# Local attention with whitening on one core: the first softmax's transposes move into image 1's infinity row, and its band transposes are held back

## Chip, cores and metric

The kernel runs on one core of one Trainium2 chip. The metric is device time in microseconds (us) of one execution; lower is better. TensorE is called PE below, VectorE DVE, ScalarE ACT, GpSimd POOL, and SP is the sync engine that issues most transfers.

## The reference

Input x has four images of 256 channels, 64 x 64. Layer 0 makes 49 attention weights for each pixel and sums the pixel's 49 neighbours with them; layer 1 whitens the channels.

```python
k = conv(x, w1, 7x7, dilation 2, padding 6) + b1        # 256 -> 128 channels
k = conv(k, w2, 1x1) + b2                               # 128 -> 49
attn = softmax(k, axis=1)
y = sum over u, v of shift(x, 2u, 2v) * attn[7u + v]    # local attention
# layer 1, in groups of 64 channels, over all pixels of all images
Sigma = EPS * I + cov(y);  P = 5 Newton steps towards Sigma^(-1/2)
out = (P * sqrt(1 / trace)) @ (y - mean) * weight + bias
```

## The kernel before

**Convolution.** The two convolutions are folded into one with 49 outputs. It is done by evaluation and interpolation, in both directions of the image: seven points 0 to 5 and infinity (INF). A *row* below is one row point `br` of one image. For a row, `row_eval` forms combinations of image rows (buffers `rb`), `col_ops` those of columns (`xh`, temporaries `ct`), `weights` the transformed filters (`wr`), and `conv_bank` multiplies them on PE in three banks (`BANKS`, `i` = 0, 1, 2) into the PSUM buffers `cv`. ACT evicts each bank to `pv`, `col_interp` interpolates columns to `zz` and `row_interp` interpolates rows to the logits, in the tile `lgx` (image 0: in `slot` 4). The bias of the logits is added by ACT on line 658. `row_interp` runs in two parts, after rows 4 and 5.

Some rows are computed by plain taps instead: `direct` walks 14 pairs of tap and channel half. Image 0 uses it for rows 0, 4, 5 and INF, the others for INF alone (`direct_inf`, whose taps come from the DRAM tile `gi` into `spare`, the third buffer of `pv`). A `direct` with `s` = 1 adds its result to the half that was there before: a copy on ACT and a sum on DVE (line 690 and the line after it). Image 1's INF row is the exception: it is called with the taps still in SBUF and accumulates in `acc`, before image 1's weights of banks 1 and 2 are prepared.

**Attention.** `soft(b, pc)` takes half the pixels of image b: PE transposes the logits, DVE takes maxima, ACT exponentiates, DVE normalizes. `move_terms` copies the result to `zt` and stores it to the DRAM tile `sd`; `load_band` reads it back, shifted, into `band` in three parts, four transfers each, and DVE block-transposes each part (line 973). `first_half(n)` and `second_half(n)` then multiply on PE the transposed image blocks with `band` (line 1020); n counts half-pixel quarters of images, four to an image.

**Order.** PE follows the order of the code (`keep_in_program_order`). On the other engines and queues a scheduler orders instructions by priority and by its own estimate of when they are ready; `high_priority` raises a block. While `strict` is set, `in_turn` keeps the DVE operations of `add`, `sub` and `madd` in code order. `later` holds ACT copies that are let go behind the next eviction of a bank 1. The list `steps` gives the order of the rows of images 1 to 3, with costs 6, 5 and 2 for the three banks of a row; the attention of earlier images is put into gaps of this list by `plan`. In image 1 the list begins with `soft(0, 0)`, three banks of its first row, and `soft(0, 1)`.

`prepare(k, i)` makes what bank i of row k needs (weights, row and column combinations) and is called while row k - 1 is multiplied. Rows 4 and 5 of image 0 leave their row-transformed filters in DRAM (`kept`); image 1 loads them to `rb[0]` when it makes its weights from them.

Of the kernel before, what the change touches and what calls it, by code (L numbers as in the profile page):

```python
# [10 lines left out]
AF = mybir.ActivationFunctionType  # L11
# [21 lines left out]
def kernel(  # L33
# [244 lines left out]

    TT, STT = nc.vector.tensor_tensor, nc.vector.scalar_tensor_tensor

    turn, strict = [None], [False]

    def in_turn(ins):


        if turn[0] is not None:
            tc.add_manual_dep(
                ins.ins,
                turn[0],
                mybir.DependencyInfo(mybir.DependencyClass.NoSync, mybir.DependencyReason.DATA),  # L290
                reason="in_turn",
            )
        if strict[0]:
            turn[0] = ins.ins.name
        return ins
# [68 lines left out]
    def weights(b, br, i, mid=None):  # L364
# [16 lines left out]
        if br == 0:  # L381
            g = [gr0[:, v] for v in range(KS)]
        elif br in kept:

            f = rb[0].rearrange("p q r c w -> p (q r c w)")[:, : KS * nk]
            if i == 0:
                nc.sync.dma_start(f, kept[br])
            f = f.rearrange("p (v a r k) -> p v a r k", v=KS, a=NCC, k=KT)
            g = [f[:, v] for v in range(KS)]
        else:  # L390
            g = [gbr[:, v] for v in range(KS)]
# [249 lines left out]
    def row_interp(b, part):  # L641

        pt = {k: zz[:K2, k] for k in range(NP)}
        lg = lgx
        if b == 0:
            lg = store[4].rearrange("p c r w -> p (c r w)")
        lg = lg[:, : SH * W].rearrange("p (r w) -> p r w", w=W)
        outs = phases(lg[:K2])
        cut = lambda t, k: t[:, k : k + Q8]
        tr = ct.rearrange("p a b -> p (a b)")[:K2, : Q9 * W].rearrange("p (q w) -> p q w", w=W)  # L650
        interpolate(pt, tr, outs, cut, part)
        if part == 0:
            done_ = ((0, outs[0]), (2, outs[2]))
        else:
            done_ = ((3, cut(pt[5], 0)), (1, outs[1]))
            logits[b] = lg
        for a, t in done_:
            nc.scalar.activation(outs[a], t, AF.Identity, bias=bias[:K2])

    logits = {}  # L660

    def direct(b, br, s, ps, w, xr=None):


        a = 3 if br == INF else 0
        order = [(v, cc) for v in sorted(range(KS), key=lambda v: abs(v - R)) for cc in range(NCC)]
        for j, (v, cc) in enumerate(order):
            d = 2 * (v - R)
            w0, w1_ = max(0, -d), min(W, W - d)
            for h in range(2):  # L670
                if xr is None:
                    xs = slots[2 * b + h].rearrange("p c (q a) w -> p a q c w", a=4)[:, a]
                else:
                    xs = xr[:, :, h]
                pe(
                    nc.tensor.matmul(  # L676
                        ps[h * HB : h * HB + KT, :, w0:w1_],
                        w[v][:, cc],
                        xs[:, :, cc, w0 + d : w1_ + d],
                        start=(j == 0),  # L680
                        stop=(j == len(order) - 1),
                        skip_group_check=True,
                    )
                )
        z = zz[:K2, br]
        if s == 0:
            with tc.high_priority():
                nc.scalar.copy(z[:, :Q8], ps[:K2])
        else:
            nc.scalar.copy(z[:, Q8], ps[:K2, Q8 - 1])  # L690
            add(z[:, 1:Q8], z[:, 1:Q8], ps[:K2, : Q8 - 1])

    def conv_psum():
        ncv[0] += 1
        return cv_buf[(ncv[0] - 1) % 2].rearrange("p (q w) -> p q w", w=W)

    def direct_inf(b):

        nc.sync.dma_start(spare[:, :NTAP], kept[INF])
        t = spare[:, :NTAP].rearrange("p (v a k) -> p v a k", v=KS, a=NCC)  # L700
        direct(b, INF, 0, conv_psum(), [t[:, v] for v in range(KS)])

    acc = ps_y.tile([P, 2, Q8, W], F32, tag="y", name="acc")
    nc.vector.memset(acc, 0.0)
    rows = [(0, br) for br in (1, 2, 3)]
    NR0 = len(rows)
    rows += [(b, br) for b in range(1, B) for br in ROWS]
    cur, nxt = {}, {}

    def prepare(k, i):  # L710

# [3 lines left out]
            cur["x"] = row_eval(b, br)  # L715
        nxt.update(w)
        col_eval(cur["x"], i)

    def conv_step(k, i):
        w = {bc: nxt.pop(bc) for bc in BANKS[i]}  # L720
# [76 lines left out]
    for i in three:  # L797
        bank(2, i)
    row_weights(4)
    keep_weights(4)  # L800
    xrs[4] = row_eval(0, 4)
    direct0(4, 0)
# [18 lines left out]
    prepare(NR0, 0)  # L821
    direct0(5, 1)
    row_interp(0, 1)

    direct(1, INF, 0, acc[:, 0], [tap[:, UPOS[3], v] for v in range(KS)])
    prepare(NR0, 1)
    prepare(NR0, 2)
    strict[0] = False
# [120 lines left out]

    BAND = ((0, 3), (3, 5), (5, 8))  # L950

    def load_band(n, part):

        if (n, part) in loaded or n not in moved:
# [4 lines left out]
        for g in range(CR):  # L959
# [6 lines left out]
                ),  # L966
            )

        f = band.rearrange("p m r w -> p (m r) w")[
            :, m0 * BP + (R if m0 == 0 else 0) : m1 * BP - (R if m1 == NCH else 0)  # L970
        ].rearrange("p e w -> p (e w)")
        with tc.high_priority():
            nc.vector.transpose(f, f)  # L973
        if (n, part) == (4 * B - 1, len(BAND) - 1):
            bring_back(dma)

# [231 lines left out]
    for b in range(1, B):  # L1208
# [4 lines left out]
                for i, cost in enumerate((6, 5, 2)):  # L1213
                    steps.append((cost, lambda k=k, i=i: conv_step(k, i)))
        if b == 1:
            steps.insert(0, (0, lambda: soft(0, 0)))
            steps.insert(4, (0, lambda: soft(0, 1)))
        else:
            steps.insert(0, (12, lambda b=b: direct_inf(b)))
        j, at, whole = 0, 0, sum(c for c, _ in steps)  # L1220
        for cost, f in steps:
            f()
            at += cost
            if at * NPC >= (j + 1) * whole:
                gap(b, j)
# [220 lines left out]
```

## Time and profile before

| quantity | value |
|---|---|
| runs | 752.46, 752.98, 753.97 us (median 752.98) |
| profiled execution: its own time, span | 753.07 us, 751.3 us |
| mean granted TensorE clock | 0.984 of full speed |
| matmul instructions, DVE, ACT | 7512, 1268, 953 |
| HBM read, written | 65.88 MB, 47.33 MB |

The profile is of one execution. A line of a timeline is: start in us from the span's start, duration in us, engine, source line, operation, tiles written and read, shape, count, and in brackets the idle time of the engine just before, with what ended it. Lines 306, 309 and 313 are the helpers `add`, `sub` and `madd`, so their operations are told apart by tiles: `xh` column combinations, `ct` their temporaries, `rb` row combinations, `wr` weights, `pv` and `zz` interpolation. Line 536 is a bank's matmuls, 676 those of `direct`, 859 the softmax's transposes, 960 the band's transfers, 973 its block transposes, 932 the store `sd<-zt`, 699 the load of INF taps.

### The profile page before, as it was taken

The page shows a single profiled execution, that of the slowest core. Times are in us where ns is not written, and L with a number is a line of the kernel's source. Part 1 is how long each engine was busy: PE and PEld are TensorE (multiplying, and loading weights), DVE is VectorE, ACT ScalarE, POOL GpSimd, SP SyncE. Part 2 cuts the span into 40 slices and gives each one's busy share as a digit, 9 for nine tenths or more (in the row PEclk, how much of TensorE's full clock was granted, in tenths as well). Part 3 has the DMA queues.
Part 4 walks back from the last instruction along what each step waited for, and adds up shares of the span by engine and source line. Part 5 has one row for each costly group of instructions (what it writes and reads, how often), then busy time and mean ns, then how long its engine had stood idle before and what let it go on. Part 6 is the DMA issues. An engine that isn't in the chain of part 4 may idle for free.

```text
span 751.3 us, 18491 instructions
## 1 busy us (share of the span) xinstructions
PE 706.7 (94%) x7512; PEld 531.5 (71%) x7512; DVE 611.5 (81%) x1268; ACT 332.3 (44%) x953; POOL 50.9 (7%) x52
## 2 busy tenths in 40 slices
PE   6999999997988997999999999999999889998996
PEld 1449643376887795599998976899998678885331
DVE  3799899998999988877997799799969665545575
ACT  1424240253564354375453443745435573322564
POOL 0410070020000110001000100000000000000000
PEclk9999999999999998999999999999999999999999
DMA  8981120127153393046743930433532243362588
GB/s 322 257 302 73 60 88 17 64 98 232 64 183 120 103 342 97 21 132 217 256 130 116 336 82 1 146 111 110 166 90 82 50 135 111 117 251 118 209 359 327
DMA packets 59629, 114.41 MB, mean 152 GB/s; under 512 B 22887, under 2 KB 42008, under 8 KB 58776
## 3 DMA queue, kind: packets, MB, share of 16 engines
q1 hardware_dynamic: 55848, 94.36, 37.7%
q0 software_dynamic: 3696, 18.88, 7.3%
q8 instruction: 59, 0.97, 0.5%
q14 instruction: 26, 0.21, 0.1%
HBM read 65.88 MB, written 47.33 MB: 151 GB/s over the span
## 4 chain that ended last, share of the span: by engine, by line
PE 60%; DVE 27%; ACT 5%; DMA 4%; issue 3%; SPq 1%; DVEq 0%; ACTq 0%
PE cv L536 18%; PE y L1020 13%; PE acc L676 6%; PE tp L1386 4%; PE sig L1073 3%; PE tp L1052 3%; PE cv L676 3%; PE tp L991 3%; DVE xh L313 3%; DVE pv L313 2%; DVE rb L313 2%; DVE zz L313 2%; DMA band<-sd 2%; DVE band L973 2%; PE cv L222 2%
## 5 line engine op out<-in xcount | busy, mean ns | idle before, releaser
L536 PE MATMUL cv<-xh,wr 128*49 128x128 f32 x4368 | 249.7, 275 | 5.9 <-DVE xh L306 5.6
L536 PEld LDWEIGHTS cv<-xh,wr 128*49 128x49 f32 x4368 | 243.6, 124 | 9.9 <-issue 7.1
L1020 PE MATMUL y<-band,xb 128*128 128x224 f32 (+2 forms) x640 | 154.6, 381 | 8.7 <-ACT xb L999 6.7
L1020 PEld LDWEIGHTS y<-band,xb 128*128 128x128 f32 x640 | 111.4, 196 | 31.4 <-ACT xb L999 9.4
L546 ACT COPY pv<-cv 113x486 f32<-113x486 f32 (+1 forms) x63 | 30.0, 476 | 84.6 <-PE cv L536 84.4
L1039 ACT ACTIVATE slot<-y,pivot 128x512 f32<-128x512 f32 x53 | 36.7, 740 | 67.5 <-PE y L1020 67.4
L1060 ACT COPY yt<-tp 128x256 f32<-128x256 f32 x128 | 45.5, 379 | 37.8 <-PE tp L1052 36.4
L973 DVE STREAM_TRANSPOSE band<-band 128x864 f32<-128x864 f32 (+1 forms) x48 | 47.6, 992 | 13.2 <-DMA band<-sd 13.1
L991 PE MATMUL tp<-ident,slot 128*128 128x128 f32 x256 | 50.0, 297 | 8.2 <-ACT yt L1060 8.2
L313 DVE SCALAR_TENSOR_TENSOR pv<-pv 113x162 f32<-113x162 f32 x186 | 55.2, 320 | 0.8 <-ACT pv L546 0.3
L1052 PE MATMUL tp<-ident,slot 128*128 128x128 f32 x256 | 52.0, 299 | 3.7 <-ACT yt L1060 1.0
L1052 PEld LDWEIGHTS tp<-ident,slot 128*128 128x128 f32 x256 | 41.2, 205 | 13.8 <-issue 4.0
L991 PEld LDWEIGHTS tp<-ident,slot 128*128 128x128 f32 x256 | 40.1, 205 | 14.8 <-ACT yt L1060 9.7
L873 ACT ACTIVATE d<-tp,mx 128x49 f32<-128x49 f32 x128 | 36.9, 337 | 21.4 <-DVE mx L868 17.9
L919 ACT COPY zt<-d 32x112 f32<-32x112 f32 (+2 forms) x156 | 44.8, 287 | 1.9
L313 DVE SCALAR_TENSOR_TENSOR xh<-ct 128x512 f32<-128x512 f32 x42 | 27.9, 685 | 13.7 <-PE cv L536 13.4
L1073 PEld LDWEIGHTS sig<-yt 128*64 128x64 f32 x1024 | 33.2, 140 | 6.4 <-issue 4.9
L1073 PE MATMUL sig<-yt 128*64 128x65 f32 x1024 | 37.7, 228 | 0.0
L999 ACT COPY xb<-tp 128x256 f32<-128x256 f32 x87 | 30.5, 375 | 14.0 <-PE tp L991 13.4
L999 DVE COPY xb<-tp 128x256 f32<-128x256 f32 x41 | 16.4, 421 | 23.4 <-PE tp L991 23.4
L676 PE MATMUL acc<-slot,tap 128*49 128x496 f32 (+3 forms) x168 | 34.6, 569 | 0.0
L873 ACT ACTIVATION_READ_ACCUMULATOR d<-tp,mx 128x1 f32 x128 | 30.8, 242 | 0.0
(222 smaller groups left out, 958.0 us busy)
## 6 DMA issues: line engine op xcount, KB each, us to landing
out_dram<-out SPq DMA_DIRECT2D x32, 512.0 KB, 3.4
sd<-zt SPq DMA_DIRECT2D x16, 896.0 KB, 4.0
slot<-in_x_dram POOLq DMA_DIRECT2D x12, 1024.0 KB, 10.1
band<-sd SPq DMA_DIRECT2D x128, 84.0 KB, 2.1
wr<-gd SPq DMA_DIRECT2D x15, 588.0 KB, 3.7
wr<-gd SPq DMA_DIRECT2D x15, 490.0 KB, 4.0
spill<-slot POOLq DMA_DIRECT2D x3, 2048.0 KB, 7.7
back<-spill SPq DMA_DIRECT2D x3, 2048.0 KB, 13.1
```

What stands on the lines that cost most here:

```text
L313: return in_turn(STT(o, a, f, b, ALU.mult, ALU.add))
L536: nc.tensor.matmul(cv[h * HB : h * HB + KT, k, sr : sr + n, sc : sc + n], wv[:, sc, sr, cc], xh[bc][:, :n, h * NCC + cc, :n], start=(j == ...
L676: nc.tensor.matmul(ps[h * HB : h * HB + KT, :, w0:w1_], w[v][:, cc], xs[:, :, cc, w0 + d : w1_ + d], start=(j == 0), stop=(j == len(order) ...
L873: nc.scalar.activation(d[:, h, i], lt[i // NI][:, i % NI, h, :KT], AF.Exp, bias=mx[:, i, h : h + 1], accum_out=s[:, h, i : i + 1],)
L919: ins = nc.scalar.copy(o, i)
L973: nc.vector.transpose(f, f)
L991: nc.tensor.transpose(t[:, cc * P : (cc + 1) * P], xt[:, cc, CR * m : CR * (m + 1), bass.ds(pc, SW, 2)], ident,)
L999: (nc.vector.tensor_copy if tail else nc.scalar.copy)(xb, t[:, :C])
L1020: nc.tensor.matmul(ps[:, cc, q0 - half * HALF : q1 - half * HALF, :], xb[:, cc * P : (cc + 1) * P], rhs, start=(k == 0), stop=(k == len(PI ...
L1052: nc.tensor.transpose(t[:, cc * P : (cc + 1) * P], yt[:, cc, CR * i : CR * (i + 1), bass.ds(pc, SW, 2)], ident,)
L1060: nc.scalar.copy(yb.rearrange("p a g c -> p (a g) c")[:, :, :GW], t[:, :C].rearrange("p (e c) -> p e c", c=GW),)
L1073: nc.tensor.matmul(sig[g * GW : (g + 1) * GW, cc], yb[:, cc, g, :GW], yb[:, cc, g], start=(count[0] == 0 and cc == 0), stop=(count[0] == 4 ...
```

## The change

- `direct` gets an argument `mid`: a function that is called half way, after 6 of the 14 pairs. Image 1's INF row becomes a `direct_inf` like the others', with taps from DRAM and a `cv` buffer, is put at the head of `steps`, and calls `soft(0, 0)` as its `mid`.
- The block transposes of the first band (n = 0) are not emitted with its transfers but kept in `held`, and released after the first row of image 1, with an order edge behind the last DVE operation of the last `prepare` (the one for bank 2 of the second row).
- The copy and the sum of row 0's second half in image 0 are kept in `seconds` and emitted after `row_weights(4)`.
- For images 1 to 3 the bias operations of the first part of `row_interp` go to `later`.
- Row 5's kept filters are loaded to `lgx` instead of `rb[0]`.

```diff
@@ -278,7 +278,7 @@
 
     TT, STT = nc.vector.tensor_tensor, nc.vector.scalar_tensor_tensor
 
-    turn, strict = [None], [False]
+    turn, strict, latest = [None], [False], [None]
 
     def in_turn(ins):
 
@@ -290,6 +290,7 @@
                 mybir.DependencyInfo(mybir.DependencyClass.NoSync, mybir.DependencyReason.DATA),
                 reason="in_turn",
             )
+        latest[0] = ins
         if strict[0]:
             turn[0] = ins.ins.name
         return ins
@@ -382,7 +383,9 @@
             g = [gr0[:, v] for v in range(KS)]
         elif br in kept:
 
-            f = rb[0].rearrange("p q r c w -> p (q r c w)")[:, : KS * nk]
+
+            f = lgx if br == 5 else rb[0].rearrange("p q r c w -> p (q r c w)")
+            f = f[:, : KS * nk]
             if i == 0:
                 nc.sync.dma_start(f, kept[br])
             f = f.rearrange("p (v a r k) -> p v a r k", v=KS, a=NCC, k=KT)
@@ -655,16 +658,25 @@
             done_ = ((3, cut(pt[5], 0)), (1, outs[1]))
             logits[b] = lg
         for a, t in done_:
-            nc.scalar.activation(outs[a], t, AF.Identity, bias=bias[:K2])
+
+            def end(a=a, t=t):
+                return nc.scalar.activation(outs[a], t, AF.Identity, bias=bias[:K2])
+
+            if b > 0 and part == 0:
+                later.append(end)
+            else:
+                end()
 
     logits = {}
 
-    def direct(b, br, s, ps, w, xr=None):
+    def direct(b, br, s, ps, w, xr=None, mid=None):
 
 
         a = 3 if br == INF else 0
         order = [(v, cc) for v in sorted(range(KS), key=lambda v: abs(v - R)) for cc in range(NCC)]
         for j, (v, cc) in enumerate(order):
+            if j == KS - 1 and mid is not None:
+                mid()
             d = 2 * (v - R)
             w0, w1_ = max(0, -d), min(W, W - d)
             for h in range(2):
@@ -687,25 +699,35 @@
             with tc.high_priority():
                 nc.scalar.copy(z[:, :Q8], ps[:K2])
         else:
-            nc.scalar.copy(z[:, Q8], ps[:K2, Q8 - 1])
-            add(z[:, 1:Q8], z[:, 1:Q8], ps[:K2, : Q8 - 1])
+
+            def second():
+                nc.scalar.copy(z[:, Q8], ps[:K2, Q8 - 1])
+                add(z[:, 1:Q8], z[:, 1:Q8], ps[:K2, : Q8 - 1])
+
+            if br == 0:
+
+                seconds.append(second)
+            else:
+                second()
+
+    seconds = []
 
     def conv_psum():
         ncv[0] += 1
         return cv_buf[(ncv[0] - 1) % 2].rearrange("p (q w) -> p q w", w=W)
 
-    def direct_inf(b):
+    def direct_inf(b, mid=None):
 
         nc.sync.dma_start(spare[:, :NTAP], kept[INF])
         t = spare[:, :NTAP].rearrange("p (v a k) -> p v a k", v=KS, a=NCC)
-        direct(b, INF, 0, conv_psum(), [t[:, v] for v in range(KS)])
+        direct(b, INF, 0, conv_psum(), [t[:, v] for v in range(KS)], mid=mid)
 
     acc = ps_y.tile([P, 2, Q8, W], F32, tag="y", name="acc")
     nc.vector.memset(acc, 0.0)
     rows = [(0, br) for br in (1, 2, 3)]
     NR0 = len(rows)
     rows += [(b, br) for b in range(1, B) for br in ROWS]
-    cur, nxt = {}, {}
+    cur, nxt, prepared = {}, {}, [None]
 
     def prepare(k, i):
 
@@ -715,6 +737,7 @@
             cur["x"] = row_eval(b, br)
         nxt.update(w)
         col_eval(cur["x"], i)
+        prepared[0] = latest[0]
 
     def conv_step(k, i):
         w = {bc: nxt.pop(bc) for bc in BANKS[i]}
@@ -797,6 +820,7 @@
     for i in three:
         bank(2, i)
     row_weights(4)
+    seconds.pop()()
     keep_weights(4)
     xrs[4] = row_eval(0, 4)
     direct0(4, 0)
@@ -821,8 +845,6 @@
     prepare(NR0, 0)
     direct0(5, 1)
     row_interp(0, 1)
-
-    direct(1, INF, 0, acc[:, 0], [tap[:, UPOS[3], v] for v in range(KS)])
     prepare(NR0, 1)
     prepare(NR0, 2)
     strict[0] = False
@@ -949,6 +971,18 @@
 
     BAND = ((0, 3), (3, 5), (5, 8))
 
+    held = []
+
+    def release_held(after):
+        for f in held:
+            tc.add_manual_dep(
+                f().ins,
+                after.ins.name,
+                mybir.DependencyInfo(mybir.DependencyClass.NoSync, mybir.DependencyReason.DATA),
+                reason="release_held",
+            )
+        held.clear()
+
     def load_band(n, part):
 
         if (n, part) in loaded or n not in moved:
@@ -966,11 +1000,18 @@
                 ),
             )
 
-        f = band.rearrange("p m r w -> p (m r) w")[
-            :, m0 * BP + (R if m0 == 0 else 0) : m1 * BP - (R if m1 == NCH else 0)
-        ].rearrange("p e w -> p (e w)")
-        with tc.high_priority():
-            nc.vector.transpose(f, f)
+        def turn_blocks():
+
+            f = band.rearrange("p m r w -> p (m r) w")[
+                :, m0 * BP + (R if m0 == 0 else 0) : m1 * BP - (R if m1 == NCH else 0)
+            ].rearrange("p e w -> p (e w)")
+            with tc.high_priority():
+                return nc.vector.transpose(f, f)
+
+        if n == 0:
+            held.append(turn_blocks)
+        else:
+            turn_blocks()
         if (n, part) == (4 * B - 1, len(BAND) - 1):
             bring_back(dma)
 
@@ -1213,13 +1254,16 @@
                 for i, cost in enumerate((6, 5, 2)):
                     steps.append((cost, lambda k=k, i=i: conv_step(k, i)))
         if b == 1:
-            steps.insert(0, (0, lambda: soft(0, 0)))
+
+            steps.insert(0, (0, lambda: direct_inf(1, lambda: soft(0, 0))))
             steps.insert(4, (0, lambda: soft(0, 1)))
         else:
             steps.insert(0, (12, lambda b=b: direct_inf(b)))
         j, at, whole = 0, 0, sum(c for c, _ in steps)
         for cost, f in steps:
             f()
+            if at + cost == 13:
+                release_held(prepared[0])
             at += cost
             if at * NPC >= (j + 1) * whole:
                 gap(b, j)
```

## The prediction

> **What bounds the kernel now.** I began with the page: how busy each engine is over the whole run.
>
> ```profile
> PE 706.7 (94%) x7512; PEld 531.5 (71%) x7512; DVE 611.5 (81%) x1268; ACT 332.3 (44%) x953; POOL 50.9 (7%) x52
> ```
>
> TensorE (PE) leads, so a change that removes no matmul can only win back idle time of PE. The table of waits, kept to PE and to DVE, says where that idle time is and what ended it (us in total, times, longest).
>
> ```profile
> PE tp L991 <- ACT yt L1060: 8.2, 8, 3.8
> PE cv L536 <- DVE xh L306: 5.6, 1, 5.6
> PE acc L676 <- DVE rb L313: 0.9, 1, 0.9
> DVE band L973 <- DMA band<-sd: 13.1, 5, 4.4
> ```
>
> The longest PE wait is a single one of 5.6 us, for an operand that VectorE (DVE) makes. PE's timeline places it at 183.1, in image 1's third row of convolutions, and shows the order of work ahead of it.
>
> ```profile
> 145.21 11.55 PE L676 MATMUL acc<-slot,tap 128*49 128x512 f32 x56
> 156.68 1.21 PE L859 MATMUL tp<-ident,slot 113*128 113x113 f32 x8
> 157.83 11.80 PE L536 MATMUL cv<-xh,wr 128*49 128x128 f32 x208
> 169.56 1.21 PE L859 MATMUL tp<-ident,slot 113*128 113x113 f32 x8
> 171.12 12.00 PE L536 MATMUL cv<-xh,wr 128*49 128x128 f32 x208 [0.35 <-ACT pv L546]
> 188.72 6.99 PE L536 MATMUL cv<-xh,wr 128*49 128x128 f32 x96 [5.59 <-DVE xh L306]
> ```
>
> First come image 1's infinity row (145.21), the first softmax's transposes (156.68) and two rows. DVE's timeline over the idle stretch gives its cause.
>
> ```profile
> 179.31 1.03 DVE L313 SCALAR_TENSOR_TENSOR pv<-pv 113x162 f32<-113x162 f32 x4
> 183.17 1.08 DVE L973 STREAM_TRANSPOSE band<-band 128x864 f32<-128x864 f32 x1 [2.82 <-DMA band<-sd]
> 185.84 1.22 DVE L306 TENSOR_TENSOR ct<-rb 128x1024 f32<-128x1024 f32 x1
> 186.97 0.83 DVE L973 STREAM_TRANSPOSE band<-band 128x640 f32<-128x640 f32 x1
> 187.94 0.68 DVE L306 TENSOR_TENSOR xh<-ct 128x512 f32<-128x512 f32 x1
> 190.61 1.07 DVE L973 STREAM_TRANSPOSE band<-band 128x864 f32<-128x864 f32 x1
> ```
>
> DVE stood still for 2.82 us before a block transpose whose data were still under way, with the operand that PE needs queued behind it. The busy times by stretch show that this was DVE's only hole there.
>
> ```profile
> 174.00:180.00 6.00, 6.00 (x109) 5.78 (x107) 6.00 (x17) 1.14 (x2) 0.00 (x0) 1.00 1.00 329
> 180.00:186.00 6.00, 3.12 (x56) 2.86 (x51) 3.18 (x12) 0.04 (x1) 0.00 (x0) 1.00 0.70 146
> 186.00:192.00 6.00, 3.28 (x34) 3.31 (x36) 6.00 (x12) 6.00 (x36) 0.00 (x0) 0.72 0.52 202
> ```
>
> The columns are PE, weight loads, DVE, ACT, POOL, granted clock, DMA share, GB/s. DVE is busy 5.7 us or more of each 6 from 126 to 264 except at 180 to 186 (one stretch at 240 has 5.47); PE idles several times in it. So **DVE bounds 122 to 264**; what DVE gains there PE gains, and after 291 PE is nearly without a gap to 683 and carries a gain on. The image 0 stage has one more pair of lines.
>
> ```profile
> 86.55 0.62 DVE L306 TENSOR_TENSOR zz<-zz,acc 113x448 f32<-113x448 f32 x1 [3.58 <-ACT zz L690]
> 98.78 11.59 PE L676 MATMUL acc<-rb,gbr 128*49 128x512 f32 x56 [0.93 <-DVE rb L313]
> ```
>
> DVE waits 3.58 us for PE's second half of row 0 (its sum), and later PE waits 0.93 us for DVE's rb.
>
> [...] after the 5.59 us the granted clock averages 0.72 over 186 to 192. [...] at 174 to 180 the share is 1.00, because weight loads and 1 MB of x run beside the band's twelve transfers, which take 5.2 us (median) to land against 2.1 on the page.
>
> **Second sums later.** The copy (0.21) and the sum (0.62) of row 0 move from before 87 to after row_weights(4). Nothing is added. DVE no longer stops 3.58 us at 83, and the sum itself leaves, so it reaches rb(4) some 3.6 us earlier (the sum returns just before it). PE's row 3 ends at 97.85 and its next work has rb and scaled weights by then: **0.93 us gained** on PE. DVE's lead beyond that is lost at 122.92, where the next such sum waits for PE (end 122.45) anyway; that wait grows from 0.85 to some 3.5. So 0.93 is what reaches 122, and both engines are that much earlier.
>
> **Taps from DRAM.** One more load of 343 KB; its two sisters land in 2.9 us. Its buffer is free once col_interp of row 3 ends at 129.1, and image 2's load of the same kind was issued at 129.25 in this trace, far ahead of its place in the code; so image 1's should land by about 132, and PE needs it at 144.3. SP's queue is empty from 105 to 144. Cost nothing; if that cover were gone (stuck behind the weight store that waits until 152.96) it would be about 12 us. Image 2's load now waits for image 1's matmuls (to 157.8), ahead of it or behind it only stores and a load that waits until 163.4: nothing.
>
> **Transposes amid infinity.** 56 matmul records of 11.55 us are cut after 6 of 14 taps; by widths (376 of 848 columns) that is 5.1 us. They end near 149.4. The last ACT bias of logits 0 ends at 151.03, now 150.1, so PE waits some 0.75 us, then 1.2 us of transposes, and 6.4 us of the rest. The first row starts at 157.8, as before: gain and stall cancel on PE, which has slack until 183. The softmax starts 6.5 us earlier (151.3 against 157.9). Its DVE and ACT work is the same and trades places with preparations that PE needs only from 163; a new wait of DVE for these transposes is bounded by 0 and 2 us (DVE is free of the logits at 149.3); I take 0. zt and band's memsets no longer wait for the infinity's taps (156.88). The store sd<-zt moves from 170.56 to about 164.
>
> **Band transposes held.** They now follow the last xh of image 1's second row, which ended at 176.77 and is 0.93 earlier: 175.8. Three transposes of 1.0, 0.76 and 1.0 us. The first two parts are there (their store is 6.5 us earlier and they landed by 183.7). The third landed at 185.8; with the same lag it lands at 179.3, and DVE is ready for it at 177.6: a stall of 1.7. Without the x load (still at 171.4, tied to the second transposes) in the middle of it the lag is shorter and the stall 0. I take **1.0 against 2.82**; the bound above is 8 (no lead at all). The third transpose also comes 1 us earlier than the operand of the third row; DVE's total is unchanged, so this counts only locally.
>
> **Late bias and kept weights in lgx.** Three images move one ACT bias pair (0.72 each) behind an eviction. The second of the pair already stood behind it in image 1 (288.02 after 284.10). ACT's own share of waits for lgx is 8.6 us, PE's 0.2. Bounds: 0.7 gained to 0.7 lost an image; taken as 0. Row 5's weights (686 KB) come into lgx instead of rb; same bytes, DVE has no wait for them now. Zero, within 0.5.
>
> **Sum.** 0.93 + 2.82 - 1.0 = 2.75 us off the profiled execution's 753.07 (span 751.3 and 1.8 around it) gives 750.3; the median of the runs lies 0.09 below the profiled one, so 750.2. Next late is DVE's own work, then at 286.4 a PE wait of 3.76 for ACT behind DVE behind a band transfer of 8.51 us; all of that follows work which shifts with it.
>
> **Rivals.**
> - *More*: no stall at the third part (3.75 us), and a half-clock window on PE's path (the twelve matmuls at 256.10 take 4.87 us against 3.18 elsewhere, those at 291.60 6.12) falls away. 746 to 748.7. For: PE idles less. [...] Chance 0.16.
> - *Given back*: the gain is swallowed at 286, where the band transfer is tied to x traffic at a share of 1.03, or by waits of DVE for the mid-infinity transposes. 752 to 753.5. Chance 0.20.
> - *Slower*: holding puts all three transposes ahead of col_interp and of the third row's operand. If the third part lands after 181.4 (177.6 + 2.82 + 0.93), DVE loses more than it wins; landing as late as before, at 185.8, costs 8.2 - 3.75 = 4.4 us, so 757. For: DMA is full there. Against: the earlier store. Chance 0.17.
> - *Not what it says*: the taps are late in SP's queue and PE stands about 12 us, of which the lead hides little: about 762. Chance 0.05.
>
> **How the numbers follow.** The forecast has 0.42 and its own range is 749 to 751.4. Within 0.2% (1.5 us, about what a measurement of this kernel can tell from no change) is the third case, 0.20; faster is 0.42 + 0.16; slower 0.17 + 0.05. The range, from the middle of the larger gain to the beginning of the slower case, is 746.6 to 754.5.
>
> **What would show it.** Right: the sum of row 0 beside row_weights(4) and no 3.58 wait; pv<-gi issued near 129; transposes near 150.2 with a PE wait under 1 us; band transposes in a block near 176 with under 2 us of waiting; PE's wait at 183 falling to about 3. Wrong: a DVE wait over 3 us at those transposes, a PE wait for gi, or the same total idle of PE between 150 and 300.

## The result, and the profile after

| comparison | kernel before | kernel changed | ratio (95% interval) |
|---|---|---|---|
| first | 751.49 (20 runs) | 751.21 (20 runs) | 0.9989 [0.9972, 1.0005] |
| again, with the first experiments | 752.99 (59 runs) | 750.38 (22 runs) | 0.9965 [0.9953, 0.9977] |

Times are medians of all runs; the ratio leaves out the runs that are more than 1.5% above the fastest of their kernel (3 of 20 and 2 of 22 of the changed kernel), so it is not the quotient of the medians.

The forecast was 750.2, 0.37% under the time shown for before. The second comparison, the larger one, has 0.35% and an interval that excludes no change; the first has 0.11% and doesn't exclude it. So the number is about right, at the edge of what can be told. The traces show that it is right for reasons that are only partly those of the prediction: a larger gain and a loss that it did not have nearly cancel, and that is in good part luck.

The profiled execution of the changed kernel took 758.40 us (span 756.6). It has a disturbance of its own: a piece of x landed at 52.48 instead of 37.18 though SP's queue issues in the same order at that point in both kernels. PE waited 7.99 us at 51.88, and from 57 to 63 it was granted a clock of 0.50. Everything after 60 us therefore comes some 10.6 us later than in an undisturbed execution; the lengths of stages that begin later are not touched by it.

Line numbers move with the edits. The helpers are now 307, 310 and 314 (before: 306, 309, 313); 539 is a bank's matmuls, 688 those of `direct`, 881 the softmax's transposes, 1009 the band's block transposes. Single kernels below differ by a few lines.

The page's row of engines:

```profile
PE 703.7 (93%) x7512; PEld 531.6 (70%) x7512; DVE 611.8 (81%) x1268; ACT 332.5 (44%) x953; POOL 59.8 (8%) x52
```

The work is the same but for POOL, whose 8.9 us more become important further down. The table of waits (us in total, times, longest):

```profile
PE cv L539 <- DVE xh L314: 9.1, 1, 9.1
PE cv L539 <- DVE xh L307: 8.0, 1, 8.0
DVE band L1009 <- DMA band<-sd: 5.6, 3, 3.0
PE tp L1032 <- ACT yt L1101: 2.3, 5, 0.6
PE cv L539 <- ACT pv L549: 3.2, 1, 3.2
```

Of the four lines of before, the wait of 5.6 for xh and the 0.9 for rb are gone, ACT's yt costs 2.3 instead of 8.2, and DVE's waits for the band fell from 13.1 to 5.6. The 8.0 is the disturbed start. The 9.1 is new, and larger than anything that went. First the part that was forecast, PE's timeline from image 1's INF row to its third row:

```profile
149.59 5.30 PE L688 MATMUL cv<-slot,gb 128*49 128x480 f32 x26
154.72 5.21 PE L688 MATMUL cv<-slot,pv 128*49 128x512 f32 x24
160.60 1.21 PE L881 MATMUL tp<-ident,slot 113*128 113x113 f32 x8 [0.67 <-ACT slot L663]
161.74 6.54 PE L688 MATMUL cv<-slot,pv 128*49 128x480 f32 x32
168.12 11.76 PE L539 MATMUL cv<-xh,wr 128*49 128x128 f32 x208
179.80 1.21 PE L881 MATMUL tp<-ident,slot 113*128 113x113 f32 x8
182.44 11.80 PE L539 MATMUL cv<-xh,wr 128*49 128x128 f32 x208 [1.42 <-issue]
197.40 2.93 PE L539 MATMUL cv<-xh,wr 128*49 128x128 f32 x28 [3.16 <-ACT pv L549]
```

INF starts at 154.72 without a wait for its taps. The first softmax's transposes stand in its middle, after a wait of 0.67. Ahead of the third row PE waits 3.16 where it waited 5.59. DVE's timeline over the same time has the held block transposes, with no bracket behind them, so without any wait:

```profile
187.00 1.79 DVE L1009 STREAM_TRANSPOSE band<-band 128x864 f32<-128x864 f32 x2
...
189.97 1.07 DVE L1009 STREAM_TRANSPOSE band<-band 128x864 f32<-128x864 f32 x1
```

What the profile names as the end of PE's 3.16 is now on ACT. Its timeline shows the exponentials of the second softmax waiting for a maximum from DVE, and PE's eviction (line 549) queued behind five pairs of them; PE goes on when that eviction ends, at 197.34:

```profile
195.37 0.30 ACT L895 ACTIVATE d<-tp,mx 128x49 f32<-128x49 f32 x1 [6.23 <-DVE mx L890]
...
196.76 0.58 ACT L549 COPY pv<-cv 113x486 f32<-113x486 f32 x1
```

The operand that ended PE's wait in the kernel before is ready hardly sooner than that: DVE finishes it at 197.30, so the eviction adds 0.04 us:

```profile
196.62 0.68 DVE L307 TENSOR_TENSOR xh<-ct 128x512 f32<-128x512 f32 x1
```

Further on, PE's timeline in image 1's sixth and last row (row point 5); the 9.13 us stand ahead of its bank 2:

```profile
279.67 4.70 PE L539 MATMUL cv<-xh,wr 128*49 128x128 f32 x80
293.50 3.52 PE L539 MATMUL cv<-xh,wr 128*49 128x128 f32 x32 [9.13 <-DVE xh L314]
```

and DVE's over that wait:

```profile
284.05 0.75 DVE L314 SCALAR_TENSOR_TENSOR zz<-zz 113x576 f32<-113x576 f32 x1
287.81 1.08 DVE L1009 STREAM_TRANSPOSE band<-band 128x864 f32<-128x864 f32 x1 [3.02 <-DMA band<-sd]
288.82 0.65 DVE L314 SCALAR_TENSOR_TENSOR lgx<-zz 113x512 f32<-113x512 f32 x1
289.39 0.68 DVE L307 TENSOR_TENSOR lgx<-zz 113x512 f32<-113x512 f32 x1
289.98 0.68 DVE L314 SCALAR_TENSOR_TENSOR xh<-rb 128x512 f32<-128x512 f32 x1
...
292.67 0.68 DVE L314 SCALAR_TENSOR_TENSOR xh<-xh,rb 128x512 f32<-128x512 f32 x1
```

The three xh operations that PE waits for stand behind the interpolation of rows 0 to 4 (zz and lgx) and behind a block transpose for `first_half(3)`, which waits 3.02 us for its data and which PE needs later than xh. In the kernel before, DVE's timeline has these xh among the zz operations, ahead of that transpose, which waits as long:

```profile
274.26 0.68 DVE L313 SCALAR_TENSOR_TENSOR xh<-rb 128x512 f32<-128x512 f32 x1
...
281.48 0.68 DVE L313 SCALAR_TENSOR_TENSOR xh<-xh,rb 128x512 f32<-128x512 f32 x1
...
286.34 1.08 DVE L973 STREAM_TRANSPOSE band<-band 128x864 f32<-128x864 f32 x1 [2.90 <-DMA band<-sd]
```

No line of the diff touches them.

To add this up I cut the span at PE's own landmarks, the starts of convolution matmuls counted from the first: **start to image 1** from the 417th to the 625th, **A** to the 1633rd (bank 2 of image 1's fifth row), **B** to the 1873rd (image 2's first row), then the rest. Idle time of PE is in brackets.

| kernel (profiled execution) | start to image 1 | A | B | rest |
|---|---|---|---|---|
| before | 71.74 (1.60) | 107.39 (12.27) | 54.35 (4.31) | 431.73 |
| changed | 71.39 (1.34) | 98.90 (7.44) | 57.94 (9.39) | 431.67 |

**A gains 8.49 us, B gives 3.59 back.** Why A gains that much can be read in the busy times by stretch. The columns are the stretch, its length, then PE, weight loads, DVE, ACT, POOL, granted clock, DMA share, GB/s. A and B in the kernel before:

```profile
157.82:265.21 107.39, 95.12 (x1293) 87.14 (x1294) 102.71 (x225) 51.62 (x177) 8.85 (x14) 0.95 0.44 139
265.21:319.56 54.35, 50.04 (x477) 37.08 (x472) 46.10 (x78) 22.82 (x54) 3.38 (x2) 0.94 0.42 142
```

and in the changed kernel without its hold (the fifth run below, whose stages are the same within 0.02 us and which has no disturbance):

```profile
157.40:256.29 98.89, 91.43 (x1294) 85.07 (x1292) 97.54 (x211) 47.86 (x149) 14.99 (x8) 0.98 0.47 152
256.29:314.22 57.93, 48.42 (x476) 36.75 (x472) 52.55 (x92) 22.86 (x53) 3.38 (x2) 0.94 0.41 137
```

DVE was busy in 102.71 of A's 107.39 us and is busy in 97.54 of 98.89. So of A's 8.5 us, 5.2 are DVE work that left A, and 3.3 are idle time of DVE (4.7 less 1.3), the forecast stall of 2.82 first. B has 6.5 us more of DVE work, so part of what A gained had only moved. Seen from PE, 4.8 of the 8.5 are idle time and 3.7 are busy time: the same matmuls at a higher clock (0.98 against 0.95).

### The profile page after: what moved, and what is told of

It is laid out like the page before. It is cut to its first block, busy times and chain, and to the rows that moved or that the text cites. A ratio compares the mean times of both kernels' runs of the same rounds, so it can differ in the third digit from the quotient of the medians.

```text
span 756.6 us, 18493 instructions
## 1 busy us (share of the span) xinstructions
PE 703.7 (93%) x7512; PEld 531.6 (70%) x7512; DVE 611.8 (81%) x1268; ACT 332.5 (44%) x953; POOL 59.8 (8%) x52
## 4 chain that ended last, share of the span: by engine, by line
PE 61%; DVE 23%; ACT 5%; DMA 5%; SPq 3%; issue 3%; DVEq 0%; ACTq 0%
PE cv L539 23%; PE y L1061 13%; PE acc L688 5%; PE tp L1430 4%; PE tp L1093 4%; PE sig L1114 3%; PE tp L1032 3%; SPq L196 3%; DMA slot<-in_x_dram 2%; DVE zz L314 2%; DVE pv L314 2%; DVE xh L314 2%; DVE rb L307 2%; DVE band L1009 2%; PE cv L688 2%
## 5 line engine op out<-in xcount | busy, mean ns | idle before, releaser
L539 PE MATMUL cv<-xh,wr 128*49 128x128 f32 x4368 | 253.7, 278 | 21.7 <-DVE xh L314 9.1
L539 PEld LDWEIGHTS cv<-xh,wr 128*49 128x49 f32 x4368 | 247.7, 125 | 26.2 <-issue 20.5
L1061 PE MATMUL y<-band,xb 128*128 128x224 f32 (+2 forms) x640 | 149.4, 372 | 6.9 <-ACT xb L1040 4.9
L1061 PEld LDWEIGHTS y<-band,xb 128*128 128x128 f32 x640 | 108.5, 191 | 27.6 <-ACT xb L1040 7.3
L688 PE MATMUL cv<-slot,pv 128*49 128x496 f32 (+3 forms) x168 | 34.9, 571 | 0.0
```

The costliest lines, as they stand in the source:

```text
L539: nc.tensor.matmul(cv[h * HB : h * HB + KT, k, sr : sr + n, sc : sc + n], wv[:, sc, sr, cc], xh[bc][:, :n, h * NCC + cc, :n], start=(j == ...
L688: nc.tensor.matmul(ps[h * HB : h * HB + KT, :, w0:w1_], w[v][:, cc], xs[:, :, cc, w0 + d : w1_ + d], start=(j == 0), stop=(j == len(order) ...
L1061: nc.tensor.matmul(ps[:, cc, q0 - half * HALF : q1 - half * HALF, :], xb[:, cc * P : (cc + 1) * P], rhs, start=(k == 0), stop=(k == len(PI ...
```

## The experiments

The comparisons are each with the runs of the kernel before on the same chip. A and B are from one profiled execution of each. The diffs are shortened.

**Run 1: the changed kernel again**, no edit.

> The changed kernel once more, for a second profile and five rounds beside the kernel before. Two stages of PE are compared: A, from image 1's first row to bank 2 of its row 4 (107.4 us before, 98.9 in the changed kernel's first profile), and B, from there to image 2's row 0 (54.4 and 58.0). Theory 'operand behind a transpose': these differences are in the order of the instructions and come back, A shorter by 6 to 9 us, B longer by 2 to 5, with one PE wait of 8 to 10 us in B for xh. Rival 'clock windows': the differences are luck with PE's half-speed windows, A and B are within 2 us of the kernel before's, and what the change is worth is the 0.9 us of row 0's later sum. Total by both: 0.3 to 1.5 us under the kernel before.

Measured: 750.38 against 752.99, ratio 0.9965 [0.9953, 0.9977]. Its profiled execution (757.94) has another disturbance, a DVE wait of 6.69 us at 240 for a band transfer; run 11 tells where that comes from. It lies in A, which is 107.91 here, so A's gain does not come back in this execution; B is 57.30, with a PE wait of 8.29 for xh. Without the disturbance A is 98.9 to 100.0 in all seven later runs that keep the transposes amid INF (2, 4, 5, 6, 7, 11 and 12).

**Run 2: the core alone.** The second sum, the bias and the buffer of row 5's weights as before; INF in `steps`, taps from DRAM, transposes amid INF and the hold as changed.

```diff
-            f = lgx if br == 5 else rb[0].rearrange(...)
+            f = rb[0].rearrange(...)
-            if b > 0 and part == 0: later.append(end)
-            else: end()
+            end()
-            if br == 0: seconds.append(second)
-            else: second()
+            second()
```

> The changed kernel without the later second sum, the late bias and the load to lgx: the infinity row with the softmax amid it, the taps from DRAM and the held transposes alone. 'Operand behind a transpose': stages A and B as in the whole change (A shorter by 6 to 9, B longer by 2 to 5), and the PE wait of 0.9 us for rb in image 0 is back, so 0.9 us slower than the whole change. 'Clock windows': no stage differs from the kernel before by more than 2 us and the time equals that of the kernel before within 0.7.

Measured: 751.62, ratio 0.9996 [0.9974, 1.0018]; A 99.04, B 57.87, PE's 0.93 us back at 97.9, and in B

```profile
283.28 3.66 PE L539 MATMUL cv<-xh,wr 128*49 128x128 f32 x32 [8.17 <-DVE xh L314]
```

The core makes both the gain of A and the loss of B, and as both return here (and in the runs below), the rival that the stages differ by luck with clock windows (stretches that were granted 0.50, as 189 to 191 was in the kernel before) is refuted. 8 of its 22 runs are above 755 us; run 11 comes back to that.

**Run 3: the later second sum alone**, put into the kernel before (the `seconds` lines of the diff and nothing else).

> The kernel before with the later second sum alone. Both theories: PE's wait of 0.93 us at 98.8 goes, 0.9 us less at the start of image 1. 'Clock windows' expects this to be all of the change: the same total as the changed kernel. 'Operand behind a transpose' expects it to be one part of two: stages A and B stay as before, and the total is 0.5 to 1.2 us under the kernel before.

Measured: 751.40 against 752.99, ratio 0.9984 [0.9973, 0.9996]; A 105.80, B 54.23. The 0.93 us are gone and the 5.4 us for xh in image 1 stay: this part is worth what it was said to be, and it is apart from the rest.

**Run 4: the operand first.** In the changed kernel, the preparation of the operand that PE waits for in B gets priority over the interpolation, and so does the same step in images 2 and 3.

```diff
+            first = b > 0 and br == ROWS[-2] and i == len(BANKS) - 1
-            prepare(k + 1, i)
+            with tc.high_priority() if first else nullcontext():
+                prepare(k + 1, i)
```

> The changed kernel, with the preparation of row 5's bank 2 (weights and xh) raised in priority, so that DVE makes it ahead of the row interpolation and of the band transpose that waits for its transfer. 'Operand behind a transpose': PE's wait of 9.1 us in stage B for xh goes, another of 3 to 5 us for ACT's yt copies may take its place as in the kernel before; total 3 to 6 us under the changed kernel, 745 to 748. 'Clock windows': within 1 us of the changed kernel. A third view, 'DVE bounds anyway': the 9.1 us are DVE's total work and only move to another wait, total within 1 us of the changed kernel with a wait as long elsewhere in stage B.

Measured: 746.83 (5 runs), ratio 0.9915 [0.9889, 0.9941]; A 98.89, B 50.63. The wait of 9 us is gone; on PE's timeline the bank runs through and the next work follows it at once:

```profile
269.06 6.47 PE L539 MATMUL cv<-xh,wr 128*49 128x128 f32 x112
275.46 0.74 PE L1095 MATMUL tp<-ident,slot 128*128 128x128 f32 x4
```

In this one execution the rest of the span took 438.9 instead of 431.7 and gave B's 7.3 us back: 3.3 are idle time of PE (with a new wait of 2.51 at 319 for ACT's yt; another, of 1.96 at 298, lies in B), the other 3.9 clock, mostly in the last 146 us, granted 0.95 where run 5 had 0.98. The medians, over several executions, keep 3.5 us against run 1. The rival that had DVE's total as the bound, with a time within 1 us of the changed kernel, is refuted by these medians; the profiled execution alone (747.62, where run 5's took 747.68) would not do it.

**Run 5: not held.** The changed kernel with the first band's block transposes emitted where its transfers are.

```diff
-        if n == 0: held.append(turn_blocks)
-        else: turn_blocks()
+        turn_blocks()
```

> The changed kernel, but the three band transposes of image 1's first half are issued as before, where their transfers are, instead of behind the third row's x operand. The prediction gave the hold the larger part of its gain (2.82 us of DVE's wait, less 1.0). 'Holding pays': DVE waits 2 to 4 us again for band<-sd in image 1's third row, PE's wait ahead of that row grows from 3.2 to 5.5 or more, stage A (98.9 in the changed kernel, 107.4 before) grows by 2.5 to 4 us; how much of it reaches the end depends on stage B, 1 to 3 us: 751.5 to 753.5. 'The earlier store pays': the store to sd stands 6.5 us earlier since the transposes lie amid infinity, so the parts are there without any hold; no DVE wait above 1 us, A within 0.7 of 98.9, and the time that of the changed kernel (750.4, within 0.7).

Measured: 749.26 against 753.02, ratio 0.9957 [0.9945, 0.9969]; A 98.89, B 57.93. DVE's timeline has the three transposes without a wait:

```profile
172.76 1.07 DVE L1009 STREAM_TRANSPOSE band<-band 128x864 f32<-128x864 f32 x1
...
175.46 0.84 DVE L1009 STREAM_TRANSPOSE band<-band 128x640 f32<-128x640 f32 x1
...
179.28 1.07 DVE L1009 STREAM_TRANSPOSE band<-band 128x864 f32<-128x864 f32 x1
```

**The hold buys nothing that can be told:** the interval overlaps that of run 1, and the stages are those of the changed kernel's first profile within 0.02 us. Here the store to `sd` is issued at 160.43 and the twelve transfers from 165.13 (before: 170.56 and 175.15); the last landed at 173.71, long before the third transpose at 179.28.

**Run 6: the third half's block transpose later.** The changed kernel and one order edge, which puts the transpose that waited 3.02 us behind image 2's x operand.

```diff
+            if (n, part) == (3, 0):
+                tc.add_manual_dep(ins.ins, latest[0].ins.name, ..., reason="third_band")
```

> The changed kernel, with one edge in DVE's order: the block transpose for the third half (the one that waited 3.02 us for band<-sd at 287.8 with the operands xh behind it) comes behind image 2's first x operand. 'Operand behind a transpose': the wait of PE in stage B falls from 8.2 to 9.1 us by the 3.0 of the wait and the 1.0 of the transpose, to 4 or 5, B from 57.9 to about 54, and the time to 746.5 to 748. The rest of that wait stays, since the rows' interpolation (lgx) still stands ahead of xh. 'DVE bounds anyway': the wait only moves to another place, the sum of A, B and the rest changes by less than 1 us: 749.5 to 751.

Measured: 746.15 (6 runs), ratio 0.9930 [0.9909, 0.9950]; B 54.73, rest 433.37, and

```profile
278.95 3.66 PE L539 MATMUL cv<-xh,wr 128*49 128x128 f32 x32 [5.09 <-DVE xh L314]
```

9.1 less 4.0 is 5.1: the wait of the transpose (3.0) and the transpose (1.0) came off PE's wait, as expected. The time is just under the 746.5 to 748 expected. In the 5.1 us that are left DVE works without a stop, on the interpolation ahead of the last xh.

**Run 7: both edits together.**

> Both edits: the priority for the preparation of image 2's first row (746.83 alone) and the edge that puts the third half's block transpose behind it. With the priority alone DVE still waited 3.38 us for the band at 274.67, with interpolation behind it, and new PE waits of 1.96 and 2.51 us for ACT's yt stood at 298 and 319. 'The remaining wait is on the path': those shrink by 2 to 3 us: 744 to 745.5. 'Off the path': PE has the operand in time by then and the interpolation is not late: 746.3 to 747.3. A loss is possible too, up to 2 us, if the transpose comes so late that the next half's products wait for it.

Measured: 744.18 (6 runs), ratio 0.9901 [0.9884, 0.9917]; B 47.42 with 0.62 of idle time, the rest 439.06. The 1.96 us wait at 298 is gone, the one at 318 stays:

```profile
318.41 0.50 PE L1041 MATMUL tp<-ident,slot 128*128 128x128 f32 x2 [2.47 <-ACT yt L1110]
```

**Run 8: the operand first, in the kernel before.** (The row whose preparation is raised is image 1's last, as in run 4; the expectations call it image 2's first row.)

> The kernel before with the same priority for the preparation of image 2's first row, nothing of the change. There xh stands among the interpolation already, and PE's wait in stage B (3.76 us at 286.44) was for ACT's yt. 'Operand behind a transpose' (the wait of 9 us is a cost of the change's new order): little to gain here, 0 to 2 us: 749.5 to 751.5, stage A unchanged at 107.4 and B 53 to 54.4. 'The priority is a gain by itself, whatever the order before': 4 us or more off B, 747 to 748.5, and the gain of the change proper is then the difference to 746.83, near nothing.

Measured: 752.47 against 753.02, ratio 0.9999 [0.9985, 1.0013]. B falls to 51.66, the rest rises to 434.46, and nothing reaches the end. So the priority is no gain in itself; in run 4 it takes back a cost that the change brought.

**Run 9: the transposes behind INF.** The changed kernel with the first softmax after the INF row, still with its taps from DRAM and the hold.

```diff
-            steps.insert(0, (0, lambda: direct_inf(1, lambda: soft(0, 0))))
-            steps.insert(4, (0, lambda: soft(0, 1)))
+            steps.insert(0, (0, lambda: direct_inf(1)))
+            steps.insert(1, (0, lambda: soft(0, 0)))
+            steps.insert(5, (0, lambda: soft(0, 1)))
```

> The changed kernel with the first softmax's transposes behind image 1's infinity instead of amid it; the taps still come from DRAM in the place where the changed kernel has them, the band transposes are still held, the second sum and the bias are still late. 'The earlier store pays' (by it the block transposes find their data, and by it VectorE's order shifts, with the 8 to 9 us of PE's wait as a side effect): the store to sd falls back to 170, the held transposes wait 1 to 3 us or the third row's operand stands behind them, stage A goes back to 104 to 107.4, stage B to 54.3 with xh among the interpolation again, and the time is that of the later sum alone, 751 to 752.5. 'The taps or the hold pay': A stays within 1 of 98.9 and B at 57.9, time within 1 of 750.4. If A stays short while B falls to 54, the time is 746 to 748.

Measured: 751.64 against 752.40, ratio 0.9988 [0.9979, 0.9996]; A 107.45, B 52.59. DVE and PE, each from its own timeline:

```profile
181.63 1.08 DVE L1009 STREAM_TRANSPOSE band<-band 128x864 f32<-128x864 f32 x1 [2.58 <-DMA band<-sd]
```

```profile
187.19 3.19 PE L539 MATMUL cv<-xh,wr 128*49 128x128 f32 x28 [5.15 <-DVE xh L307]
```

The stall is back although the transposes are held, A is that of the kernel before, in B DVE's xh and block transposes stand in the places that they had before, and what remains of the gain is the size of run 3. **Moving the transposes amid INF makes A's gain and B's loss.** Which estimate of the scheduler moves DVE's order in B is not shown.

**Run 10: as run 9, and not held.**

> As the run before it, and the band transposes not held either: of the change only the taps from DRAM, the later sum and the late bias are left. 'The hold pays where the store is late': VectorE waits 2.8 us again for band<-sd in image 1's third row and PE 5.6 for xh, A is 106 to 107.4, and the time is 1 to 3 us above that of the run with the hold: 752 to 754. 'The hold is worth nothing in either order': the two agree within 0.7.

Measured: 751.81, ratio 0.9991 [0.9981, 1.0001]; A 107.03, DVE's wait 2.78. Against run 9 the hold is worth nothing in this order either. The edge lets the transposes go behind an operand of the second row, and in both runs DVE reached them at 179.1, two to three us before their data.

**Run 11: the bias and the buffer back.** The changed kernel with the first two edits of run 2's diff, the second sum late.

> The changed kernel with the bias not late and row 5's weights loaded into rb as before. The prediction put both at nothing (0, within 0.5 to 0.7 an image). 'Nothing': stages A and B within 0.7 of 98.9 and 57.9 and the time within 0.8 of 750.4. 'They pay': up to 0.7 an image late in A or in the rest, 751.2 to 752.5. The other side: the bias late costs, 749 to 749.6.

Measured: 757.30 against 752.40, ratio 1.0026 [1.0001, 1.0050]; 16 of its 22 runs are above 755 us, against 2 of 22 in run 1, 5 of 20 in the first comparison and 8 of 22 in run 2. The other six are between 747.17 and 750.59, no slower than the changed kernel. None of the theories had this. A is 99.14, but B is 66.00. POOL's, SP's and DVE's timelines have the chain (POOL copies on lines 413 and 414 for bank 0 of a row, on 423 for bank 1):

```profile
242.85 11.69 POOL L413 COPY wr<-rb 128x196 f32<-128x196 f32 x1 [15.23 <-DMA rb<-g5d]
...
255.23 0.34 POOL L423 COPY wr<-rb 128x196 f32<-128x196 f32 x1
```

```profile
238.47 0.34 SPq L390 DMA_DIRECT2D rb<-g5d  x1
...
255.31 0.32 SPq L437 DMA_DIRECT2D gd<-wr  x1
255.72 7.97 SPq L991 DMA_DIRECT2D band<-sd  x7
```

```profile
265.87 0.84 DVE L1006 STREAM_TRANSPOSE band<-band 128x640 f32<-128x640 f32 x1 [10.79 <-DMA band<-sd]
```

A copy that elsewhere takes 0.35 us took 11.69. The store of the weights waits for the copies, the band's transfers stand behind the store on SP's queue, and DVE stands 10.79 us for them; PE then waits 7.17 and 7.83 us. In run 5, with row 5's weights in `lgx`, they are loaded at 156.63 instead of 238.47 (`rb` is free only when row 4's weights are made), and POOL's timeline shows the same copy done in 0.35 us at 240.44; the long one, of 9.46 us, is a later copy that nothing urgent waits for:

```profile
240.44 0.35 POOL L413 COPY wr<-lgx 128x196 f32<-128x196 f32 x1 [13.39 <-PE cv L539]
240.73 0.90 POOL L414 COPY wr<-lgx 128x196 f32<-128x196 f32 x1
244.93 9.46 POOL L423 COPY wr<-lgx 128x196 f32<-128x196 f32 x1 [3.30 <-PE cv L539]
```

The same thing in the copy for row 4 (13.16 us) is the disturbance of run 1's profiled execution. That the other runs above 755 us have it too is likely and not shown: only profiled executions have traces. The trace points to the buffer; the bias was undone with it, and the two were not tried apart.

**Run 12: the second softmax of image 0 one bank later**, in the version of run 7.

```diff
-            steps.insert(4, (0, lambda: soft(0, 1)))
+            steps.insert(5, (0, lambda: soft(0, 1)))
```

> The version with both edits (744.18), and the second softmax of image 0 one bank later: behind the first bank of image 1's second row instead of ahead of it. There PE waits 1.44 us at 170.4 right behind those transposes and 2.1 us at 177.4. 'The second softmax is in the way there': one or both of these waits go, A from 98.9 to 96 or 97, time 741.5 to 743.5. 'Only moved': the waits come back a bank later, or the second half's band comes late by as much, 743.7 to 745.5.

Measured: 743.51 (4 runs), ratio 0.9881 [0.9865, 0.9897], the lowest of all, though its interval overlaps that of run 7. PE's timeline now has one wait in place of the two, and names its cause:

```profile
171.75 7.17 PE L539 MATMUL cv<-xh,wr 128*49 128x128 f32 x96 [2.57 <-DVE xh L307]
```

It begins at the same moment as in run 7, 171.85 there, where the record says only "issue": PE waited for xh then too. The transposes had filled part of that wait. A is 99.98, 1.1 us longer than in run 7 and not the 96 to 97 of the first view, and the rest 2.3 shorter; a gain over run 7 is not shown.

## Why the prediction was right, and where it was not

- **Second sums later, 0.93 us.** Right: the PE wait is gone in every kernel with this part, and it is back in run 2. Alone it brings 0.16% [0.04, 0.27], 0.3 to 2.0 us.
- **Taps from DRAM, nothing.** Right. The load was issued at 138.76 in an execution that ran some 10.6 us late from its start, so at 128 against the forecast 129; no wait for it. The rival that PE stands for the taps is refuted.
- **Transposes amid INF, 0.75 of wait that the slack absorbs.** The wait is 0.67. DVE got a new one of 1.01 (a reciprocal behind ACT's exponentials), within the 0 to 2 given and above the 0 taken. The store came 10.1 us earlier than before in run 5 (160.43), where the step had 6.5 (about 164). The first row started at 157.4 in run 5, against the 157.8 forecast.
- **Held transposes, 2.82 less 1.0.** The stall went whole, 2.82 for 0, but not through the hold. The failed step is the landing of the third part, put at 179.3: it landed by 173.7, 3.6 us because the store was earlier than forecast and 2.0 because store to landing took 13.3 us instead of 15.2. The prediction had the earlier store in its text, and made it a helper of the hold; runs 5, 9 and 10 show that the store, and not the hold, ends the stall.
- **PE's wait at 183 falling to about 3.** Right: 3.16. The profile names an eviction on ACT as its end, but the xh is ready only 0.04 us before that, so what is left of xh's delay accounts for the wait, as forecast.
- **Bias and buffer, zero within 0.5.** Wrong in the new order: without them the median is 757.3. The step looked only at who waits for `lgx` and `rb` in the kernel before, where POOL's first copy for row 5 took 0.46; it did not ask when those copies would run in the new order, and against what. In the old order they do seem to be worth nothing: runs 9 and 10, with them, have 0.9988 and 0.9991, run 3, without them, 0.9984.
- **All that follows shifts with it.** This sentence is the largest miss. DVE's order in B was made anew, and PE waits 9.1 us there for an operand behind a transpose and an interpolation. The prediction knew that DVE bounds this part of the run, yet it priced DVE's order as fixed outside the moved instructions. A's gain was put at under 3 us and is 8.5; B's loss was not there and is 3.6. The stages of the two profiled kernels differ by -0.35 - 8.49 + 3.59 - 0.06 = -5.3 us, in single executions; the medians of the runs by 2.6 (run 1). The gap between the two is within the spread of the executions: apart from the two above 755, the runs of the changed kernel in run 1 reach from 746.6 at a mean clock of 0.991 to 751.9 at 0.982, with the same program.
- **The sign "the same total idle of PE between 150 and 300".** The prediction named it as one of being wrong, and it came: 16.6 us before, 16.8 in the changed kernel (160.6 to 310.6, for its late start) and 17.0 in run 5. The wait of 9.1 took up what the other waits gave. The other two signs did not come.

Of the rivals, *More* has its mechanism right in A: there is no stall at the third part, and 3.7 us of the gain are clock, which the forecast, counting on idle time of PE alone, left out. *Given back* is true in the main: a gain was swallowed near 286, by DVE's order, not by the x traffic that it named. They nearly cancel, so that the forecast came out is in good part luck.

## What to carry to other kernels

Where a scheduler orders an engine by its estimates, an edit in one stage can reorder another: compare the order of that engine's instructions over the whole program before pricing anything as "shifts with it". An operand that the leading engine needs next should not stand behind an instruction that waits for a transfer; one priority and one order edge on such a place took another 6.2 us off the changed kernel by the medians (750.38 to 744.18), or some 4.8 by the ratios (0.9965 to 0.9901), about twice what the change itself had (2.6). When a part is said to cost nothing because nobody waits for its buffer now, ask what it keeps early, and take it out once to see.

## What the runs showed of the hardware

**Some POOL copies took 9 to 14 us beside DVE work without a pause.** In run 11 all DVE records from 241.64 on are two-operand forms on SBUF tiles and each begins before the one ahead of it ends, until a gap of 0.03 us at 254.32 to 254.35; the copy that began at 242.85 ended at 254.54. In run 5 the copy of 9.46 us ended at 254.39 after a gap at 254.18 to 254.21; in run 1 the copy of 13.16 ended at 240.17, after DVE had stopped at 239.97. In the changed kernel one of 13.16 us ended at 120.16 after a gap at 119.95 to 119.99. The kernel before has such a copy too, of 13.99 us at 97.18, which ended at 111.17 after a gap at 110.97 to 111.00. Each of these ends about 0.2 us after DVE's first pause. That DVE holds these copies up is read from the times alone. The copy that passed in 0.35 us in run 5 ran beside a block transpose (239.78 to 240.84), which reads one tile. But two-operand instructions without a pause do not always go with a long copy. In the changed kernel they fill DVE from 233.54 to 241.13, and three copies follow each other there, of 0.62, 0.81 and 0.47 us (the pair of DVE's `rb` operations at 235.94 takes 1.44 us beside them, where it took 1.29 in the kernel before). The first of the three is

```profile
236.21 0.62 POOL L413 COPY wr<-rb 128x196 f32<-128x196 f32 x1 [52.84 <-PE tp L1093]
```

What decides between the two is open; no run was made for this alone.

**The granted clock was 0.50 in short stretches during or after waits of PE.** In A the kernel before had three of them, 189 to 191, 237 to 239 and 257 to 260, which follow PE waits of 5.59, 2.18 and 1.23 us. The changed kernel had one there, 198 to 201, after the wait of 3.16. The twelve matmuls into `y` that took 4.87 us at 256.10 in the kernel before took 3.18 at 259.32 in the changed one, where the clock was 1.00. In B of the changed kernel the stretches 288 to 294 and 294 to 300, at and after the wait of 9.1 us, were granted 0.50 and 0.77. Of the 8.5 us that A gained, 3.7 were clock; in the kernel before PE's longest waits in A were 5.59, 2.18 and 1.79 us, in the changed one 3.16, 1.42 and 1.35. Which waits are followed by such a stretch is not shown: after the 1.79, which ended at 212.49 in the kernel before, 213 to 219 was granted 1.00.
